# A bank rule in the list plan of a four-layer graph kernel, and less TensorE work in its first and last units

## The chip, the cores and the metric

The kernel runs on one core of a Trainium2 chip. The metric is the time on the device in microseconds (us), the median of three runs. Everything is computed in 32-bit floats.

The engines are named as in the profile: PE is the matrix engine (TensorE; PEld are its weight loads), DVE the vector engine, ACT the scalar engine, POOL GpSimd, and SP the engine that only issues transfers (DMAs). PSUM is the memory that PE writes its products to. It has eight banks of 128 x 512 floats; ACT and DVE read it.

## The reference

The input `x` has 64 graphs of 256 nodes with 128 features; one symmetric 0/1 matrix `adj` (256 x 256) is common to all. Four layers follow one another, each as `x = layernorm(x + layer(x))`:

- Layer 0: `h = x @ others_weight`; scores from sums of pairs of entries of `h @ a1` and `h @ a2`, leaky with 0.1, masked by `adj`, softmax over axis 1; the result is `att @ h + x @ self_weight`.
- Layer 1: `h = x @ W`; scores `leaky(h @ a_src + h @ a_dst)` for pairs of nodes, masked by `adj` with loops, softmax, `elu(attn @ h)`.
- Layer 2: five steps of a gated cell. In a step, `m = adj @ h` (it stands for both halves of the gate's input), `z` and `r` are sigmoids of `m` and `h`, `hv = tanh(m @ W5 + (r * h) @ U5)`, and `h = (1 - z) * h + z * hv`.
- Layer 3: `x @ W0 + sum over k = 1, 2, 3 of (adj^k @ x) @ (Wk + W(k+3))`.

## The kernel before

**Units and lanes.** Two graphs make a unit, so there are 32 units (`NU`), numbered from 0. A unit goes through layer 0 to 3 (`layer0` to `layer3`, lines 708 to 1176) on its own set of buffers, a lane. There are 10 lanes; a lane's next unit starts when its last one is done. So work of up to ten units is in flight.

**Feature-major and node-major.** Layer 2 needs the state turned from nodes-on-partitions to features-on-partitions and back in every step. There are two ways. On PE: four transposes into a bank (`feature_major`, L593; in the steps L1031) and one copy by ACT (L595, L1034). Or away from PE: one DVE transpose of 32 x 32 blocks (L606, L1006, L1019), one transfer to a buffer in DRAM (`hb`) and four back (L612, L1012). `far(u, step)` chooses: true is away from PE. `FIRST_FAR` gives the first step that is far in one of the first units, `LAST_FAR` the first that is not in one of the last, counted from the end (0 is unit 31). All other units are far in all steps.

**Products with adj.** After a far turn the product with `adj` is the fast one (`left_fast`, L885 to L939): three sums on POOL (L893 to L896), seven 128 x 128 products on PE (L904), two ACT copies (L916, L919), four DVE adds (L925 to L939). After a turn on PE it is the plain one (`left`, L881): four products of 256 columns and one ACT copy (L959). The gates follow (L963: products of 512 columns; L975, L984, L993: ACT; L978, L991, L996, L998: DVE).

**Loads of x.** Units below `XDIRECT` load `x` in one transfer (L364) and turn it on PE (L593, L595). The others load it in four transfers of quarter blocks with rows of 32 floats (L368) and turn it with one DVE transpose (L714).

**Layer 0's row terms.** For units below `DIRECT_D` the score's column term is computed on PE (four small products, L752); for the others a row is written to DRAM (`rowu`, L620), read back in two pieces (L743) and added (L746).

**Layer 3.** `layer3_blocks` (L1064 to L1146) computes it in 128 x 128 blocks: 21 products (L1088), POOL sums (L1080, L1121 to L1123), ACT copies (L1099) and DVE adds (L1102, L1135). The last `PLAIN` units use `layer3_end` (L1148 to L1172): 12 products of 256 columns (L1157, L1164) that hold two banks, two ACT copies (L1161). The last two units end with `layernorm_last` (L683 to L702).

**Dummy products.** `warm(WARM, ...)` puts products of the identity (L405) behind unit 0's layer 1, with the rank of a 33rd unit, so that they go only where PE has nothing else. Four more stand at the very start.

**The order.** `Plan` records every instruction as a task with an engine, an assumed duration, and what it reads and writes; then `Plan.run` lays out an order for all engines at once by simulating them: whenever an engine is free, it takes the ready task with the smallest key (`first`) among those for which there are free banks (`fits`). A key is the unit times `PERIOD` plus the task's due time; a due time adds up durations and latencies along what the task depends on, times `PACE` (`PACE_GATED` in layer 2). `HASTE` lowers the key of a task within the life of a bank that its unit holds, by engine. `START` is the time up to which other, shorter latencies are assumed; `TURN` delays a DVE instruction[...]; `MARGIN` lengthens assumed durations of an engine; `R2` and `R3` rank the setup of layers 2 and 3. The instructions are then issued in that order; the engines run it with the waits that the data and the banks need. Two tasks of one group (parts of one bank, say) have no dependence on each other in the plan.

Of the kernel before, what the change touches and what calls it, by code (L numbers as in the profile page):

```python
# [25 lines left out]
SMALL = ("ve", "cu", "d", "elu", "shift")  # L26
TIGHT = 4
HALVES = 0
DIRECT_D = 3
WARM = 6  # L30
FIRST_FAR = {0: 2, 1: 2}
LAST_FAR = {0: 1}
PERIOD = 41000.0
TAIL = 0.3
LATE = 5
PACE = 4.0
PACE_GATED = 1.56
HOLD = 80
DIRECT_ROWS = 3
XDIRECT = 10  # L40
START = 35e3
HASTE = {"pe": 45000.0, "act": 45000.0}
IN_PSUM = (0, 1, 0, 1)
MARGIN = {}
TURN = 12000.0
PLAIN = 4
R2 = 1
R3 = 1.5


class Cell:


    def __init__(self, ap=None, bank=False, over=(), seeded=False, full=False):
        self.ap, self.bank = ap, bank
        self.seeded, self.full = seeded, full

        self.over = list(over)
        for c in over:
            c.over.append(self)  # L60
        self.writers, self.readers, self.users = [], [], 0
        self.group, self.waits = None, set()


class Task:
# [9 lines left out]
class Plan:  # L75
# [2 lines left out]

    LATENCY = {"pe": 400, "dve": 350, "act": 350, "pool": 900, "sp": 4000}

    EARLY = {"pe": 250, "dve": 180, "act": 200, "pool": 250, "sp": 2500}
    OWN = {"pe": 0, "dve": 70, "act": 70, "pool": 100}
# [9 lines left out]
    def add(self, eng, ns, fn, reads=(), writes=(), after=(), wait=0, group=None, dma=False, port=False):  # L94
        dma = dma or eng == "sp"
        t = Task(eng, ns if dma or self.unit < 0 else ns * MARGIN.get(eng, 1.0), fn, self.unit, wait, dma)
        t.base = ns
# [25 lines left out]

    def seen_at(self, t, by):
        return t.end if t.eng != by.eng or t.dma else t.off + self.OWN[t.eng]

    def fits(self, t):
        seeded = sum(c.seeded for c in t.takes)
        return len(t.takes) <= len(self.free_banks) and seeded <= sum(self.full[id(b)] for b in self.free_banks)
# [26 lines left out]
    def run(self, spawn, units, key):  # L156

        queue, done_at, order = list(units), {}, []
        open_units, lane_of = {}, {}
        ready = {e: [] for e in ("pe", "dve", "act", "pool", "sp")}  # L160
        free = dict.fromkeys(ready, 0.0)
        held, twice = dict(dve=0.0, pool=0.0), False
        seen, now, running = 0, 0.0, []

        def enlist():
            nonlocal seen
            for t in self.tasks[seen:]:
                open_units[t.unit] = open_units.get(t.unit, 0) + 1
                t.left = 0
                for d in t.deps:  # L170
                    if d in done_at:
                        t.at = max(t.at, self.seen_at(d, t))
                    else:
                        t.left += 1
                        d.then.append(t)
                if not t.left:
                    ready[t.eng].append(t)
            seen = len(self.tasks)

        def start(lane):  # L180
            mine = [u for u in queue if u % LANES == lane]
            if mine:
                self.unit, self.step = mine[0], 0
                queue.remove(self.unit)
                lane_of[self.unit] = lane
                spawn(self.unit, lane)

                for t in self.tasks[seen:]:
                    t.due = max([d.due + (PACE_GATED if t.layer == 2 else PACE) * (d.ns + (
                        d.wait + self.LATENCY["sp" if d.dma else d.eng] if d.dma or d.eng != t.eng else self.OWN[t.eng]))  # L190
                        for d in t.deps if d.unit == t.unit], default=0.0)
                self.hold(self.tasks[seen:])
                enlist()

        enlist()
        for lane in range(LANES):
            start(lane)
        while any(ready.values()) or running:

            for t in [t for t in running if t.end <= now]:  # L200
                running.remove(t)
                for c in t.banks:
                    c.users -= 1
                    if not c.users:
                        self.full[id(c.ap)] = c.full
                        self.free_banks.append(c.ap)
                open_units[t.unit] -= 1
                if not open_units[t.unit] and t.unit in lane_of:
                    start(lane_of[t.unit])
            for e, tasks in ready.items():  # L210
                if free[e] > now:
                    continue

                fit = [t for t in tasks if t.at <= now + (HOLD if now < START else 0) and self.fits(t)]
                if not fit:
                    continue
                t = min(fit, key=lambda t: key(t) + (TURN if twice and t.port and e == "dve" else 0))
                if t.at > now:
                    continue
                tasks.remove(t)  # L220
                self.take(t)
                order.append(t)
                begin = now
                if t.port:
                    begin = max(now, held["pool" if e == "dve" else "dve"])
                free[e] = t.off = begin + t.ns
                if e == "dve":
                    twice = t.port
                if t.port:
                    held[e] = t.off - 65 if e == "dve" else begin + 50 if t.ns > 900 else t.off - 125  # L230
                t.end = t.off + (self.EARLY if now < START else self.LATENCY)["sp" if t.dma else e] + t.wait
                done_at[t] = t.end
                running.append(t)
                for n in t.then:
                    n.left -= 1
                    n.at = max(n.at, self.seen_at(t, n))
                    if not n.left:
                        ready[n.eng].append(n)
            times = [t.end for t in running] + [f for f in free.values() if f > now]
            times += [t.at for tasks in ready.values() for t in tasks if t.at > now]  # L240
            times = [x for x in times if x > now]
            if not times:
                assert not any(ready.values()), "the plan is stuck"
                break
            now = min(times)
        assert not queue and len(order) == len(self.tasks)
        return order
# [3 lines left out]
def kernel(  # L251
# [108 lines left out]
    def load_x(u, by="sp"):  # L360
        z = lanes[u % LANES]["m"]
        if u < XDIRECT:
            queue = {"sp": nc.sync, ACT: nc.scalar}[by]
# [69 lines left out]
    def blocks(name):  # L433

        whole = Cell(sb(name, [P, 2 * NC, N]))
        return whole, Cell(whole.ap[:, 0:NC])
# [63 lines left out]

    plan.rank = R2

# [41 lines left out]

    plan.rank = R3
    w3f, base = blocks("w3")
# [26 lines left out]
    def gd(ap):  # L573
        return ap.rearrange("p (g d) -> p g d", g=G)
# [10 lines left out]
    def far(u, step):  # L585


        return step >= FIRST_FAR.get(u, -1) and step < LAST_FAR.get(NU - 1 - u, STEPS + 1)

    def feature_major(src, view, t):  # L590
        ps = bank()
        for g in range(G):
            add(PE, 110, lambda g=g: nc.tensor.transpose(ps.ap[:, g * P : (g + 1) * P], view(g), ident.ap),  # L593
                (src, ident), (ps,))
        add(ACT, 475, lambda: nc.scalar.copy(t.ap, ps.ap), (ps,), (t,))  # L595
# [31 lines left out]
    def on_all(u, t, row, src, view):  # L627


        if u >= DIRECT_ROWS:  # L630
            to_row(row, src, view, G)
            from_row(t, row)
            return t, lambda: t.ap.rearrange("q (p b c) -> q b c p", b=UB, c=NC)
        ps = bank()
        for g in range(G):
            add(PE, 110, lambda g=g: nc.tensor.transpose(  # L636
                ps.ap[:, g * P : (g + 1) * P], view()[:, g : g + 1].to_broadcast([P, P]), ident.ap), (src, ident), (ps,))
        return ps, lambda: ps.ap.rearrange("q (b c p) -> q b c p", b=UB, c=NC)
# [70 lines left out]
    def layer0(u, L):  # L709
        xT, z = L["xT0"], L["m"]  # L710
        if u < XDIRECT:
            feature_major(z, lambda g: gd(z.ap)[:, g], xT)
# [23 lines left out]
        row, rv = on_all(u, lc, L["row"], cu, lambda: cu.ap[:, 2])  # L736
        if u >= DIRECT_D:
            to_row(L["rowu"], cu, lambda: cu.ap[:, 0:2].rearrange("p k g -> p (k g)"), 2 * G)
# [77 lines left out]
    def layer1(u, L):  # L816
# [48 lines left out]
        if not u:  # L865
            plan.rank = NU
            warm(WARM, [plan.tasks[-1]])
            plan.rank = None
# [177 lines left out]
    def layer3(u, L):  # L1046
# [10 lines left out]

        if u >= NU - PLAIN:
            layer3_end(u, L, xT, aT, s, tail)
# [123 lines left out]
    def first(t):  # L1183
        if t.rank is not None:
            return t.rank * PERIOD
        if t.unit < 0:
            return t.due - 1e6
        soon = HASTE.get(t.eng, 0) if t.within else 0
        return (t.unit if t.unit < NU - LANES else NU - 1 - LATE - (NU - 1 - t.unit) * TAIL) * PERIOD + t.due - soon
# [34 lines left out]
```

The softmax here doesn't subtract the row's maximum and nothing guards it: scores larger than these inputs give would overflow.

## Time and profile before

| what | us |
| --- | --- |
| median of 3 runs (1382.1 to 1382.66) | 1382.4 |
| the profiled execution | 1382.03 |
| its span, first to last instruction | 1380.2 |
| PE busy | 1371.9 |
| DVE busy | 1167.7 |
| ACT busy | 972.2 |
| POOL busy | 691.3 |

The granted clock of PE is 1.0 of its full speed. A group's row has line, engine, operation, output and inputs with their shapes, the count, then busy time in us, the mean of one in ns, then the idle time of the engine just before and what ended most of it. A 32-bit product is two matmul records in the trace, a transpose is one. Matmuls overlap in their pipeline, so that the mean of one is longer than the distance from one to the next. Numbers in tile names are left out: `ps` is any bank.

### The profile page before, as it was taken

What the parts mean: (1) busy time and instruction counts of PE and PEld (TensorE: products, weight loads), DVE (VectorE), ACT (ScalarE), POOL (GpSimd) and SP (SyncE); (2) the same over time, 40 slices, a digit from 0 to 9 for tenths busy, and PEclk for the clock granted to TensorE, in tenths of its full rate; (3) what the DMA queues carried; (4) which work ended last, traced back from release to release, by engine and by line L of the source; (5) the groups of instructions that cost most, each with busy time, mean ns of one, the idle gap of its engine ahead of it and who ended that gap; (6) DMA issues with size and microseconds to landing.
All of it is one profiled execution on the core that took longest, in us unless ns stands there. A gap on an engine that the chain in (4) does not pass through costs nothing.

```text
span 1380.2 us, 24466 instructions
## 1 busy us (share of the span) xinstructions
PE 1371.9 (99%) x7221; PEld 970.5 (70%) x7221; DVE 1167.7 (85%) x2709; ACT 972.2 (70%) x2414; POOL 691.3 (50%) x1240
## 2 busy tenths in 40 slices
PE   9999999999999999999999999999999999999998
PEld 9767676676676776767767667776666676667777
DVE  7968988988888888899888998888888787889854
ACT  6897676756776777778777767788766656566555
POOL 5214473544554664556545564565545433446814
PEclk9999999999999999999999999999999999999999
DMA  4223454454455455454555455545555443645412
GB/s 128 56 55 89 105 117 114 98 126 106 107 131 108 92 117 137 109 118 105 109 126 119 112 111 110 109 107 134 119 114 117 90 103 84 131 111 117 109 47 69
DMA packets 530084, 147.21 MB, mean 107 GB/s; under 512 B 456480, under 2 KB 495136, under 8 KB 529952
## 3 DMA queue, kind: packets, MB, share of 16 engines
q1 hardware_dynamic: 529152, 145.13, 46.8%
q8 instruction: 58, 0.95, 0.3%
q14 instruction: 74, 0.61, 0.2%
q10 hardware_dynamic: 800, 0.52, 0.1%
HBM read 81.10 MB, written 64.46 MB: 105 GB/s over the span
## 4 chain that ended last, share of the span: by engine, by line
PE 98%; DVE 1%; ACT 0%; issue 0%; POOL 0%; POOLq 0%; DVEq 0%; ACTq 0%
PE ps L963 50%; PE ps L904 20%; PE ps L1088 10%; PE ps L840 4%; PE ps L803 4%; PE ps L727 2%; PE ps L852 2%; PE ps L798 2%; PE ps L881 1%; PE ps L1157 1%; PE ps L1164 0%; PE ps L405 0%; PE ps L593 0%; PE ps L1031 0%; PE ps L636 0%; PE ps L752 0%
## 5 line engine op out<-in xcount | busy, mean ns | idle before, releaser
L963 PE MATMUL ps<-m,gT 128*128 128x512 f32 x960 | 473.3, 593 | 0.0
L963 PEld LDWEIGHTS ps<-m,gT 128*128 128x128 f32 x960 | 168.0, 191 | 131.8 <-issue 114.4
L975 ACT ACTIVATE e<-ps,bias 128x512 f32<-128x512 f32 x160 | 109.8, 687 | 94.7 <-PE ps L963 85.8
L649 POOL TENSOR_SCALAR ve<-st 128x4 f32<-128x4 f32 x110 | 26.8, 244 | 278.4 <-DVE st L647 269.6
L963 PE MATMUL ps<-e,u5T 128*128 128x512 f32 x320 | 163.5, 592 | 0.0
L904 PEld LDWEIGHTS ps<-adjTp,ht 128*128 128x128 f32 x726 | 118.6, 191 | 61.2 <-issue 48.6
L652 POOL TENSOR_TENSOR rstd<-ve,nhalf 128x4 f32<-128x4 f32 x126 | 137.5, 1091 | 47.5 <-DVE ve L649 41.4
L993 ACT ACTIVATE p<-ps,bias 128x512 f32<-128x512 f32 x160 | 109.9, 687 | 66.6 <-PE ps L963 64.2
L904 PE MATMUL ps<-adjTp,e 128*128 128x128 f32 x968 | 149.0, 276 | 0.2 <-ACT m L919 0.2
L984 ACT ACTIVATE ps<-ps,bias 128x512 f32<-128x512 f32 x160 | 105.6, 661 | 55.1 <-PE ps L963 54.3
L893 POOL TENSOR_TENSOR e<-ht 128x256 f32<-128x256 f32 x121 | 96.9, 801 | 88.1 <-DMA ht<-hb 73.1
L904 PEld LDWEIGHTS ps<-adjTp,e 128*128 128x128 f32 x968 | 129.6, 192 | 11.9 <-issue 7.9
L996 DVE SCALAR_TENSOR_TENSOR ps<-ps,p 128x512 f32<-128x512 f32 x160 | 110.2, 689 | 32.0 <-ACT p L993 31.4
L904 PE MATMUL ps<-adjTp,ht 128*128 128x128 f32 x726 | 136.7, 275 | 0.0
L963 PEld LDWEIGHTS ps<-e,u5T 128*128 128x128 f32 x320 | 58.7, 190 | 63.1 <-issue 55.5
L963 PE MATMUL ps<-xT,gT 128*128 128x512 f32 x192 | 98.2, 593 | 0.0
L671 ACT ACTIVATE x<-ht,ve,rstd 128x128 f32<-128x128 f32 x208 | 91.1, 490 | 5.1 <-POOL ve L660 5.0
L936 DVE TENSOR_TENSOR m<-ps,m 128x256 f32<-128x256 f32 x182 | 74.8, 413 | 14.1 <-PE ps L904 12.8
L829 ACT ACTIVATE e<-m,esd 128x256 f32<-128x256 f32 x116 | 84.6, 769 | 0.0
L978 DVE SCALAR_TENSOR_TENSOR e<-e,xT 128x512 f32<-128x512 f32 x96 | 72.2, 752 | 12.9 <-ACT e L975 12.4
L893 POOL TENSOR_TENSOR e<-x 128x256 f32<-128x256 f32 x61 | 48.6, 797 | 65.5 <-ACT x L671 57.7
L919 ACT COPY m<-ps 128x128 f32<-128x128 f32 x182 | 48.0, 268 | 44.0 <-PE ps L904 35.0
(219 smaller groups left out, 3356.1 us busy)
## 6 DMA issues: line engine op xcount, KB each, us to landing
hb<-p SPq DMA_DIRECT2D x182, 256.0 KB, 2.3
ht<-hb SPq DMA_DIRECT2D x484, 64.0 KB, 2.6
xT<-hb SPq DMA_DIRECT2D x244, 64.0 KB, 2.6
m<-row SPq DMA_DIRECT2D x58, 256.0 KB, 3.7
hb<-p SPq DMA_DIRECT2D x124, 64.0 KB, 1.8
ht<-hb SPq DMA_DIRECT2D x31, 256.0 KB, 2.8
out_dram<-x SPq DMA_DIRECT2D x30, 256.0 KB, 2.4
m<-in_x_dram SPq DMA_DIRECT2D x88, 64.0 KB, 2.4
```

What stands on the lines that cost most here:

```text
L652: add(POOL, 1010, lambda: nc.gpsimd.tensor_tensor(rstd.ap, ve.ap, nhalf.ap, op=ALU.pow), (ve, nhalf), (rstd,))
L671: add(ACT, 400, lambda j=j, b=b, ch=ch, view=view, at=at, shift=shift, col=col: nc.scalar.activation(X[u].ap[:, b, ch, :], view()[:, j, :] ...
L829: add(ACT, 660 if u >= DIRECT_ROWS else 360, lambda g=g, b=b: nc.scalar.activation(e.ap[:, g, :].rearrange("p (c n) -> p c n", c=NC), ev() ...
L893: add(by, wide, lambda: eng.tensor_sub(four[:, 0:2], blk(slice(2, 3)).to_broadcast([P, 2, D]), blk(slice(0, 4, 3))), (src,), (s,), group=s ...
L904: add(PE, mm_ns(P) + 4, lambda: nc.tensor.matmul(ps.ap[:, at * P : (at + 1) * P], lhs(), mat.ap[:, k, c * P : (c + 1) * P], start=start, s ...
L936: add(DVE, 335, lambda: nc.vector.tensor_tensor(mv[:, 1:3], pv(y)[:, 0:2], mv[:, 3:4].to_broadcast([P, 2, P]), op=ALU.add), (y, m), (m,))
L963: add(PE, mm_ns(T), lambda: nc.tensor.matmul(ps.ap, w(), rhs.ap, start=start, stop=stop, skip_group_check=True), (c, rhs), (ps,), after)
L975: add(ACT, 590, lambda ps_g=ps_g, up=up, tr=tr: nc.scalar.activation(tr.ap, ps_g.ap, AF.Tanh, bias=bias2.ap[:, 1:2], scale=0.5 / up), (ps_ ...
L984: add(ACT, 590, lambda ps_g=ps_g, up=up, tz=tz: nc.scalar.activation(tz.ap, ps_g.ap, AF.Tanh, bias=bias2.ap[:, 0:1], scale=0.5 / up), (ps_ ...
L993: add(ACT, 590, lambda ps_v=ps_v, up=up, tv=tv: nc.scalar.activation(tv.ap, ps_v.ap, AF.Tanh, bias=bias2.ap[:, 2:3], scale=1 / up), (ps_v, ...
L996: add(DVE, 600, lambda tz=tz, tv=tv, vv=vv: nc.vector.scalar_tensor_tensor(vv.ap, tz.ap, 1.0, tv.ap, op0=ALU.add, op1=ALU.mult), (tv, tz), ...
L1088: nc.tensor.matmul(part(ps, at)[:, 0], l(), r(), start=start, stop=True, skip_group_check=True)
```

## The change

The planner gets a rule: a task that uses a bank is taken only when no instruction of another engine that used this bank (as far as it is the same cell, one use of a bank from its first writer to its last reader) is still unfinished in the simulated time. Each cell keeps the end of the last task of each engine (`last`), and `settled` asks for it. Apart from that, constants change: which turns and which products stay on PE in the first and last units, how `x` of units 5 to 9 is loaded and turned, how unit 2's column term is computed, which form layer 3 has in units 28 and 29, how many dummy products there are, and the constants of the order. The order of all engines is laid out anew from them.

```diff
-DIRECT_D = 3
-WARM = 6
-FIRST_FAR = {0: 2, 1: 2}
-LAST_FAR = {0: 1}
+DIRECT_D = 2
+WARM = 3
+FIRST_FAR = {0: 2, 1: 1}
+LAST_FAR = {0: 3}
 PERIOD = 41000.0
 TAIL = 0.3
 LATE = 5
-PACE = 4.0
+PACE = 3.0
 PACE_GATED = 1.56
 HOLD = 80
 DIRECT_ROWS = 3
-XDIRECT = 10
-START = 35e3
-HASTE = {"pe": 45000.0, "act": 45000.0}
+XDIRECT = 5
+START = 25000.0
+HASTE = {"pe": 70000.0, "act": 70000.0, "dve": 70000.0}
 IN_PSUM = (0, 1, 0, 1)
-MARGIN = {}
-TURN = 12000.0
-PLAIN = 4
-R2 = 1
-R3 = 1.5
+MARGIN = {"pool": 1.1}
+TURN = 1000.0
+PLAIN = 2
+R2 = 1.3
+R3 = 2.0
...
         self.group, self.waits = None, set()
+        self.last = {}
...
-    LATENCY = {"pe": 400, "dve": 350, "act": 350, "pool": 900, "sp": 4000}
+    LATENCY = {"pe": 400, "dve": 350, "act": 350, "pool": 900, "sp": 3500}
...
+    def settled(self, t, now):
+
+        return not any(e != t.eng and end > now for c in t.banks for e, end in c.last.items())
+
...
-                fit = [t for t in tasks if t.at <= now + (HOLD if now < START else 0) and self.fits(t)]
+                fit = [t for t in tasks if t.at <= now + (HOLD if now < START else 0) and self.fits(t) and self.settled(t, now)]
...
                 done_at[t] = t.end
+                for c in t.banks:
+                    c.last[e] = t.end
```

## The prediction

> **What bounds the kernel now.** I read the page's busy line and the chain that ended last, then a table of stages, then the order of TensorE (PE) in the first and last units, and last the groups of waits on ACT and DVE. First the page:
>
> ```profile
> span 1380.2 us, 24466 instructions
> ...
> PE 1371.9 (99%) x7221; PEld 970.5 (70%) x7221; DVE 1167.7 (85%) x2709; ACT 972.2 (70%) x2414; POOL 691.3 (50%) x1240
> ...
> PE 98%; DVE 1%; ACT 0%; issue 0%; POOL 0%; POOLq 0%; DVEq 0%; ACTq 0%
> ```
>
> PE is busy for all but 8.3 us of the span and is 98% of the chain. Busy can hide a stall, so I also took the distance from one matmul record's start to the next: a 512-column record steps 0.429 us (chain row: L963 x16 in 6.87), a 256-column one 0.216 (L881 x16 in 3.46), a 128-column one 0.111 (L904 x16 in 1.78), a transpose 0.11 (L1031 below: 4 from 1351.62 to 1352.06). An f32 product is two such records, a transpose one. All 7221 records at those steps come to about 1366 us. With 1.3 us before the first matmul and 5.6 after the last one's end (1374.65), about 7 us of stalls are left: 3 in the first 10 us, some 4 in the remaining 1364. So PE's order has almost nothing left to give; what PE no longer has to do is the only large term. The stages (columns: length, then busy PE, PE load, DVE, ACT, POOL, clock, DMA share, GB/s):
>
> ```profile
> 10.00:20.00 10.00, 10.00 (x90) 9.87 (x87) 9.23 (x28) 6.24 (x21) 8.56 (x20) 1.00 0.75 207
> 20.00:30.00 10.00, 10.00 (x92) 10.00 (x91) 8.65 (x31) 7.83 (x24) 6.08 (x12) 1.00 0.04 4
> 30.00:36.00 6.00, 5.93 (x45) 5.49 (x44) 4.54 (x17) 4.64 (x15) 2.01 (x2) 1.00 0.35 75
> 36.00:48.00 12.00, 12.00 (x82) 10.99 (x81) 11.97 (x39) 10.50 (x29) 3.81 (x8) 1.00 0.17 31
> 48.00:60.00 12.00, 12.00 (x58) 8.47 (x57) 11.69 (x34) 10.70 (x30) 1.51 (x2) 1.00 0.34 67
> ...
> 1340.00:1370.00 30.00, 30.00 (x158) 25.19 (x157) 15.61 (x42) 15.52 (x39) 13.95 (x31) 1.00 0.21 54
> ```
>
> DVE is full from 36 to 60 us, and PE full beside it; at the end PE is full and DVE half idle. PE's own order in the first units and near the end:
>
> ```profile
> 28.53 1.91 PE L593 MATMUL ps<-ident,m 128*128 128x128 f32 x16
> ...
> 36.35 3.79 PE L727 MATMUL ps<-wx,xT 128*128 128x133 f32 x32
> 39.97 1.03 PE L405 MATMUL ps<-ident 128*128 128x256 f32 x4
> ...
> 42.67 0.59 PE L405 MATMUL ps<-ident 128*128 128x256 f32 x2
> ...
> 1351.62 0.60 PE L1031 MATMUL ps<-ident,p 128*128 128x128 f32 x4
> ```
>
> L405 is the dummy product with the lowest rank: from 40 to 48 us PE had nothing else ready. So the "full" PE of 36 to 48 us is filled, partly with dummies, partly with the first work of units 6 to 9 (L593, L727), while DVE sets the pace.
>
> **What the Trainium skill says.** "PSUM — Partial Sum Buffer", section on bank collisions: two engines may not use one bank at once, even at different columns, and have to be kept apart by bank. The trace agrees: the groups below wait for an instruction with which they share a bank and no data (L671 and L808 both read layer 0's product; L925 and L919 both read the bank x of the fast product). "TensorE: Matmul & The Clock Gate", section "Wait — 56ns, not 53.3ns?": N/2.4 + 2.5 ns a matmul; the 0.429 us of a 512-column record is that with the columns passed twice (426.7 + 2.5). "Perfetto Trace Analysis", section "Identifying the Most-Contended Engine": matmul busy share tells little of headroom; hence the start-to-start account above. "DMA: Bandwidth & Descriptors", section "Why small descriptors are slow (HBM only)": small pieces cost an overhead each; the turned load reads rows of 128 bytes where the plain one reads 512, and the DMA share is already 0.75 at 10 to 20 us.
>
> ```profile
> L671 ACT ACTIVATE x<-ps,ones,rstd 128x128 f32<-128x128 f32 x112 | 44.9, 463 | 8.5 <-DVE esd L808 5.7 <-POOL rstd L652 2.2 <-DVE ht L873 0.5
> L919 ACT COPY m<-ps 128x128 f32<-128x128 f32 x182 | 48.0, 268 | 44.0 <-PE ps L904 35.0 <-DVE m L925 8.0
> L925 DVE TENSOR_TENSOR m<-ps,e 128x128 f32<-128x128 f32 x182 | 50.5, 281 | 33.1 <-PE ps L904 19.0 <-ACT m L919 12.6
> ```
>
> **The change, part by part.**
>
> XDIRECT 10 to 5: units 5 to 9 lose 4 PE transposes each, 20 x 0.11 = 2.20 us of PE, and a copy on ACT, 5 x 0.588 = 2.9. They gain a DVE transpose (L714, 0.699), 5 x 0.70 = 3.5 us, and four 64 KB loads for one of 256 KB: 15 more issues on SP at about 0.5 us (L368 x2 in 1.01), so SP ends its loads at about 22 us and not 14.7. DVE's idle time from 10 to 36 us is 26 - 22.4 = 3.6 us, just the 3.5 that is added, if the loads are there in time; otherwise it lands in the stretch in which DVE is full.
>
> DIRECT_D 3 to 2: unit 2 loses 8 records at 0.107 (8 from 11.32 to 12.18), 0.86 us of PE. Its score goes by rowu (lands in 1.8), then two reads of it (3.0), queued behind those loads: d at 22 + 0.5 + 1.8 + 1.2 + 3.0, about 29 us, where DVE's L766 of unit 2 now starts at 22.8. What is late next is its max, exponential and product L803 (32.8 and 35.5 now), about 6 us; the rows of unit 3 (27.5 now) are behind the same loads but after 22.
>
> WARM 6 to 3: 6 records x 0.216 = 1.30 us of PE that only fills.
>
> FIRST_FAR of unit 1 and LAST_FAR of unit 31: three turns less on PE, 12 x 0.11 = 1.32 us. Three plain products (8 x 0.216 = 1.73) become fast ones (14 x 0.111 = 1.55): 3 x 0.17 = 0.52. ACT loses three copies of 0.59 and three of 0.58 and gains six of 0.27; DVE gains 3 x (0.70 + 0.28 + 0.41 + 0.28 + 0.41) = 6.2, POOL 3 x 1.9, SP 3 x 5 issues. At the end DVE and POOL have room; for unit 1, at about 70 us, DVE is at 31 of 40 us. Latency of a turn: 0.7 on DVE, 2.3 to land in hb, 2.6 for the last of four reads, with about 2.5 of issue, some 8 us for 1.4 before; the fast product is about 2 longer than the plain one.
>
> PLAIN 4 to 2: units 28 and 29 take the block form, 42 x 0.112 = 4.70 for 24 x 0.216 = 5.18: 2 x 0.48 = 0.96 us. More copies, adds and POOL sums, on engines that are half idle there.
>
> The bank rule (settled, last) and the constants of the order (PACE, START, HASTE, TURN, MARGIN, R2, R3, the latency of SP) remove no instruction. The waits that the rule foresees exist already, 26 us on ACT and DVE in the rows above, but off PE's path. On PE all stalls from 100 to 1300 us come to about 4 us net; a better order may gain 3 of them, and a worse one has no natural end: 1% of the span is 14 us. I take a gain of 0.5.
>
> Sum of PE work: 2.20 + 0.86 + 1.30 + 1.32 + 0.52 + 0.96 = 7.16 us. Of it 4.36 (first three) lies before 48 us, where PE is partly filled, and 2.80 where PE is full of work. The 2.80 I count whole. Of the 4.36 the dummies' 1.30 buys nothing (idle in their place), and of the other 3.06 I count 2.2: those transposes and products stood in PE's order ahead of real work, but less filler means some new idle time. So 2.80 + 2.2 + 0.5 = 5.5 us: span 1374.7; with the 1.8 us around it (1382.03 - 1380.2) 1376.5; the median is 0.4 above that run, so 1376.9, say **1377**.
>
> **Rivals.** A difference of 0.2%, 2.8 us, is about what a measurement tells from none: faster is under 1379.6, slower over 1385.2.
>
> (1) Everything counts and stalls shrink too: 7.2 + 2.5, 1372.7. For it: the order knows waits it did not know. Against: it knew nearly nothing of them and PE still lost only 4 us.
>
> (2) The head takes back what was removed there: PE idles for the 4.4 us, and L727 of units 5 to 9 (32 records, 3.6 us at 36 us) comes later since x is turned later, leaving another 0 to 3.6 us open. Then 2.8 less 0 to 3.6: 1379.6 to 1383.2, no difference. For it: the dummies at 40 to 48 us and DVE at 11.97 of 12. Here also the case that the bank rule changes only waits that PE never feels.
>
> (3) Slower, by the tail: unit 31's steps end now at 1310.8, 1323.7, 1337.7, 1351.7 (its transposes), 13 to 14 us a step, and each step has only about 2 us of slack (its PE, ACT and DVE work in a row is near 9 us and ten hand-overs of about 0.3 are 3). Two turned steps add about 2 x (6.6 + 2) = 17 us to this chain. It costs nothing while unit 31 is started that much earlier and layer 3 of other units (L1088, L1157) fills PE. If it isn't, PE runs dry at the end: the slide is 17 less what the earlier start and some 8 us of slack absorb; from 8.3 us of slide on (5.5 + 2.8) the kernel is slower, at 17 it is 1394. Against it: at 1340 to 1370 PE is without a gap, so fill exists.
>
> (4) Slower, by a worse middle: stalls of 9 us or more in place of 4, 1386 to 1390.
>
> **How the numbers follow.** The forecast's own case 0.42 (1374 to 1379.6), rival 1 0.18, rival 2 0.18, rival 3 0.12, rival 4 0.10. Faster 0.60, same 0.18, slower 0.22. The range leaves out about half of the cases 3 and 4 at the top and a little of 1 at the bottom: 1371.5 to 1387.
>
> **What would show it.** PE records go from 7221 to 7229: 20 + 8 + 6 + 12 fewer, and 3 x (14 - 8) and 2 x (42 - 24) more, short ones for long ones, with PE busy about 1365. L593 has 32 records, L405 14, L752 16, L881 56, L1157 32, L1031 20, L714 27 on DVE. Right: no PE gap in the last 70 us and under 3 us of new idle time before 60 us. Wrong: PE below 90% at 20 to 50 us (rival 2), after 1330 us (rival 3), or PE waits spread from 100 to 1300 us (rival 4). A head that runs faster because unit 0's chain got a better order would beat the forecast.

## The result and the profile after

The changed kernel takes 1374.7 us (1374.17 to 1375.07, four runs) against 1382.5 us (four runs) before: a ratio of 0.9944, 95% interval 0.9926 to 0.9961. That is 7.8 us less, clear of the noise, inside the range, and 2.3 us below the forecast. The page of the changed kernel (lines after the added code are 7 higher: L970 was L963):

```profile
span 1373.3 us, 24671 instructions
...
PE 1361.0 (99%) x7229; PEld 964.4 (70%) x7229; DVE 1181.2 (86%) x2744; ACT 965.5 (70%) x2419; POOL 701.0 (51%) x1263
...
PE 96%; DVE 2%; ACT 1%; SPq 1%; DMA 0%; issue 0%; POOL 0%; POOLq 0%; DVEq 0%
```

PE is still 99% busy and nearly the whole chain. Nothing in this page tells where 7 us of span went, so one account is used from here on, worked out from the start times of all matmul records of a trace. The *step* of a record is what it takes in a dense row (its columns twice at 2.4 GHz plus 2.6 ns, at least 111 ns for 128 columns); the sum of all steps is *PE's work*. A start more than 25 ns later than the step before it allows is a *late start*; how late these starts are is added up by stage. A late start can be a wait or a step at a lower clock. The rest are late starts below 25 ns, about 3 us in each kernel, and the 1.3 us before the first matmul. Of the first stage, 3.0 us before and 2.6 after lie in the first 10 us, where the first records of 256 columns step 0.427 us.

| kernel (profiled run), us | PE's work | late, 0-60 | late, 60-400 | late, 400-1300 | late, after 1300 | after last matmul | span |
| --- | --- | --- | --- | --- | --- | --- | --- |
| before | 1359.6 | 3.7 | 0.9 | 5.6 | 0.5 | 5.6 | 1380.2 |
| after | 1352.3 | 7.7 | 0.0 | 2.1 | 0.1 | 6.7 | 1373.3 |

So 7.3 us of work went, the first 60 us took 4.0 back, the rest of the order gave 4.8 (0.9 + 3.5 + 0.4), and the end took 1.1: 7.0 of span. (This profiled run is the slowest of its four, and that of before, 1382.03, lies below the four that it is compared with: hence 7.8 in the medians.) From 100 to 1300 us, 52 starts were late before, by 6.6 us in all and none by more than 0.54; after, 8 are, by 2.1 us, half of it one wait for the transfer of a turn (in the table of PE's waits: total us, times, longest):

```profile
PE ps L911 <- DMA ht<-hb: 0.9, 1, 0.9
```

The stages after:

```profile
36.00:48.00 12.00, 10.63 (x62) 8.42 (x60) 11.93 (x40) 9.42 (x29) 4.69 (x7) 1.00 0.41 99
48.00:60.00 12.00, 11.25 (x51) 7.90 (x52) 12.00 (x35) 12.00 (x35) 0.40 (x2) 1.00 0.14 41
...
1340.00:1370.00 30.00, 26.57 (x169) 23.29 (x168) 16.41 (x52) 18.79 (x53) 16.59 (x34) 1.00 0.24 62
```

At 36 to 48 us PE has 1.4 us of open gaps beside a full DVE, where it had none; at 48 to 60 us ACT is full as well (in the last row PE simply ends at 1366.6). PE's order there:

```profile
37.37 1.46 PE L412 MATMUL ps<-ident 128*128 128x256 f32 x6
...
41.69 2.06 PE L810 MATMUL ps<-ht,p 128*128 128x130 f32 x16 [1.08 <-DVE ht L792]
...
48.75 0.65 PE L643 MATMUL ps<-ident,esd 128*128 128x128 f32 x4 [1.04 <-DVE esd L815]
```

The filler of units 6 to 9 (L734, L727 before) is used up by 35 us; then come the three dummies, then PE waits for DVE. The waits for an engine that shares a bank and no data, in the table of waits after (total us, times, longest):

```profile
ACT m L926 <- DVE m L932: 6.8, 9, 2.0
DVE m L932 <- ACT m L926: 0.8, 3, 0.3
DVE esd L815 <- ACT x L678: 0.4, 2, 0.3
```

Before they were 8.0, 12.6 and 1.7 us, and 5.7 of ACT for esd, which has gone: 28.0 us fell to 8.0. So the plan does what it says.

### The profile page after: what moved, and what is told of

The parts are those of the page before. It is cut to its first block, busy times and chain, and to the rows that moved or that the text cites. A ratio compares the mean times of both kernels' runs of the same rounds, so it can differ in the third digit from the quotient of the medians.

```text
span 1373.3 us, 24671 instructions
## 1 busy us (share of the span) xinstructions
PE 1361.0 (99%) x7229; PEld 964.4 (70%) x7229; DVE 1181.2 (86%) x2744; ACT 965.5 (70%) x2419; POOL 701.0 (51%) x1263
## 4 chain that ended last, share of the span: by engine, by line
PE 96%; DVE 2%; ACT 1%; SPq 1%; DMA 0%; issue 0%; POOL 0%; POOLq 0%; DVEq 0%
PE ps L970 49%; PE ps L911 21%; PE ps L1095 10%; PE ps L810 4%; PE ps L847 4%; PE ps L805 2%; PE ps L859 2%; PE ps L734 2%; PE ps L888 1%; PE ps L1164 1%; DVE st L654 0%; SPq L619 0%; PE ps L412 0%; DVE e L765 0%; DMA xT<-hb 0%
## 5 line engine op out<-in xcount | busy, mean ns | idle before, releaser
L970 PE MATMUL ps<-m,gT 128*128 128x512 f32 x960 | 479.2, 593 | 0.0
L970 PEld LDWEIGHTS ps<-m,gT 128*128 128x128 f32 x960 | 165.7, 191 | 119.4 <-issue 100.6
L659 POOL TENSOR_TENSOR rstd<-ve,nhalf 128x4 f32<-128x4 f32 x126 | 133.7, 1061 | 64.6 <-DVE ve L656 53.1
L970 PE MATMUL ps<-e,u5T 128*128 128x512 f32 x320 | 163.5, 592 | 0.0
L911 PE MATMUL ps<-adjTp,e 128*128 128x128 f32 x992 | 153.8, 275 | 0.0
L911 PEld LDWEIGHTS ps<-adjTp,e 128*128 128x128 f32 x992 | 133.9, 192 | 11.1 <-issue 10.5
L911 PE MATMUL ps<-adjTp,ht 128*128 128x128 f32 x744 | 140.1, 275 | 0.9 <-DMA ht<-hb 0.9
L656 POOL TENSOR_SCALAR ve<-st 128x4 f32<-128x4 f32 x110 | 30.9, 281 | 193.7 <-DVE st L654 185.3
L970 PEld LDWEIGHTS ps<-e,u5T 128*128 128x128 f32 x320 | 58.7, 190 | 62.7 <-issue 51.4
L678 ACT ACTIVATE x<-ht,ve,rstd 128x128 f32<-128x128 f32 x216 | 95.1, 492 | 5.1 <-POOL ve L667 4.3
L970 PE MATMUL ps<-xT,gT 128*128 128x512 f32 x192 | 98.3, 593 | 0.4 <-DMA xT<-hb 0.4
L943 DVE TENSOR_TENSOR m<-ps,m 128x256 f32<-128x256 f32 x185 | 76.3, 414 | 9.9 <-PE ps L911 8.6
L946 DVE TENSOR_TENSOR m<-ps,m 128x256 f32<-128x256 f32 x185 | 75.8, 413 | 1.1
```

Source lines behind the costliest of these rows:

```text
L659: add(POOL, 1010, lambda: nc.gpsimd.tensor_tensor(rstd.ap, ve.ap, nhalf.ap, op=ALU.pow), (ve, nhalf), (rstd,))
L678: add(ACT, 400, lambda j=j, b=b, ch=ch, view=view, at=at, shift=shift, col=col: nc.scalar.activation(X[u].ap[:, b, ch, :], view()[:, j, :] ...
L911: add(PE, mm_ns(P) + 4, lambda: nc.tensor.matmul(ps.ap[:, at * P : (at + 1) * P], lhs(), mat.ap[:, k, c * P : (c + 1) * P], start=start, s ...
L943: add(DVE, 335, lambda: nc.vector.tensor_tensor(mv[:, 1:3], pv(y)[:, 0:2], mv[:, 3:4].to_broadcast([P, 2, P]), op=ALU.add), (y, m), (m,))
L970: add(PE, mm_ns(T), lambda: nc.tensor.matmul(ps.ap, w(), rhs.ap, start=start, stop=stop, skip_group_check=True), (c, rhs), (ps,), after)
```

## The experiments

**Theories.** A: the bank rule removed the late starts in the middle. B: the new constants of the order did. C: any new order differs by chance. Each kernel here makes the order anew, so each is also a draw; two of them change nothing but that, and their expectations name this D. Diffs over several lines are given in short form, and late starts are those of one execution of each kernel.

*The rule alone out of the changed kernel:*

```diff
-... and self.fits(t) and self.settled(t, now)]
+... and self.fits(t)]
```

> The changed kernel with the bank rule alone taken out of the planner; all constants stay. Theory A (the rule removed the stalls in the middle): the matmul steps from 100 to 1300 us again hold about 4.6 us more stall than in the changed kernel (net excess -0.8 there, +3.8 before), so 1374.7 + 4.6 = 1379.3 us. Theory B (the constants of the order did it): middle as in the changed kernel, 1374 to 1376 us. Theory C (any new order differs by chance): anywhere from 1373 to 1380 us, with the stalls at other places.

Measured 1392.4 us (ratio to before 1.0068, 1.0051 to 1.0085). This is above all three theories. The late starts from 100 to 1300 us grow by 7.3 us, where A said 4.6, but head and end grow with them. The bank waits are back at 22.9 us (9.0, 5.2, 6.6, 2.1).

*The rule alone into the kernel before:*

```diff
-... and self.fits(t)]
+... and self.fits(t) and self.settled(t, now)]
```

> The kernel before with the bank rule alone put in; all constants stay. Theory A: the middle loses its 3.8 us of net stall and head and tail stay, 1382.5 - 4.6 = 1378 us. Theory B: no change, 1381.5 to 1383.5 us, with some 50 stalls over 25 ns between 100 and 1300 us as before. Theory C: 1378 to 1386 us.

Measured 1389.4 us (1.0051, 1.0036 to 1.0066): slower, against all three. The bank waits fell to 8.0 us all the same (4.6, 0.9, 0.9, 1.6). So these waits are not what PE's late starts hang on by themselves.

*Only the six constants that take work off PE, in the kernel before:*

```diff
-DIRECT_D = 3, WARM = 6, FIRST_FAR[1] = 2, LAST_FAR = {0: 1}, XDIRECT = 10, PLAIN = 4
+DIRECT_D = 2, WARM = 3, FIRST_FAR[1] = 1, LAST_FAR = {0: 3}, XDIRECT = 5, PLAIN = 2
```

> The kernel before with only the six constants that take work off PE (DIRECT_D, WARM, FIRST_FAR, LAST_FAR, XDIRECT, PLAIN); no rule, old constants of the order. All theories: PE's ideal work falls by 7.4 us. If the head takes back what is removed there (4.1 us more stall before 60 us, as in the changed kernel), and the middle keeps its stalls: 1382.5 - 7.4 + 4.1 + about 1 of tail = 1380 us. If the head only idles because of the new order, 1375 us.

Measured 1413.6 us (1.0225, 1.0209 to 1.0240), 33 us above what was expected. PE's work is down by the same 7.3 us, and the kernel is 31 us slower: 10.2 us of late starts in the head, 23.5 at the end. The end is the prediction's tail rival, in PE's order of this kernel (L1031 and L593 are unit 31's transposes):

```profile
1386.69 1.02 PE L963 MATMUL ps<-e,u5T 128*128 128x512 f32 x2
1390.01 0.66 PE L1031 MATMUL ps<-ident,p 128*128 128x128 f32 x4 [2.30 <-DVE p L998]
1394.64 1.63 PE L593 MATMUL ps<-ident,x 128*128 128x128 f32 x4 [3.98 <-ACT x L671]
1396.07 2.83 PE L881 MATMUL ps<-adjT,x 128*128 128x256 f32 x8
```

Unit 31 is alone at the end, and PE waits for its last step (2.30) and its normalization (3.98). In the changed kernel the step's transposes stand at 1350.93, with layer 3 of other units around them, and the late starts after 1300 us sum to 0.1 us.

*Only the constants of the order, in the kernel before:*

```diff
-PACE 4.0, START 35e3, HASTE pe, act 45000, MARGIN {}, TURN 12000, R2 1, R3 1.5, sp 4000
+PACE 3.0, START 25e3, HASTE pe, act, dve 70000, MARGIN pool 1.1, TURN 1000, R2 1.3, R3 2.0, sp 3500
```

> The kernel before with only the constants of the order (PACE, START, HASTE, TURN, MARGIN, R2, R3, the latency of SP); no rule, and PE's work as before. Theory A: the middle keeps about 4 us of net stall, 1382 us. Theory B: the middle loses them, 1378 us. Theory C: 1378 to 1386 us.

Measured 1390.3 us (1.0057, 1.0042 to 1.0072), mostly in the head (9.4 us late). None of the three had it.

*Nothing but an order made anew, after and before:*

```diff
-PERIOD = 41000.0
+PERIOD = 41200.0
```

> The changed kernel with PERIOD 41200 in place of 41000 (0.5%): same rule, same work, same other constants, only an order made anew. Theory D (each order is a draw: the stalls of an order hang on small things, and the kernel as changed stands at a good draw): PE's work stays, the stalls grow by 5 to 15 us at other places, 1379 to 1390 us. Theory A' (rule and constants together make good orders as such): within 2 us of the changed kernel, 1373 to 1377 us.

> The kernel before with PERIOD 41200 in place of 41000: only an order made anew. Theory D: 1387 to 1395 us, like the single parts of the change. Theory A': within 2 us of the kernel before, 1380.5 to 1384.5 us.

Measured 1376.1 us on the changed kernel and 1392.5 us on the kernel before (1.0072, 1.0055 to 1.0088). The first follows A', the second D: 0.5% in one constant costs the kernel before 10 us, with 8.2 us of late starts at the end. Beside this one neighbour, its order was a lucky one.

*The head's three constants set back in the changed kernel:*

```diff
-DIRECT_D = 2, WARM = 3, XDIRECT = 5
+DIRECT_D = 3, WARM = 6, XDIRECT = 10
```

> The changed kernel with the head's three constants set back (XDIRECT 10, DIRECT_D 3, WARM 6): 4.4 us more PE work before 48 us. By the account of the head (4.1 us more stall in the changed kernel took back what was removed): the work comes back, the stalls before 60 us fall from 7.6 to about 3.6, the rest as in the changed kernel, so 1375 us. If those stalls come from the new order: 1379 us. Theory D adds 5 to 15 us of stalls anywhere.

Measured 1378.9 us (0.9974, 0.9963 to 0.9984). The late starts before 60 us fall from 7.7 to 4.5, as expected; but 2.6 us come up at 100 to 400 us, and the total is where the other theory had it. So the removed 4.4 us of head work do cost some 3.2 in late starts, and the order's draw decides what remains.

*The tail's two constants set back in the changed kernel:*

```diff
-LAST_FAR = {0: 3}, PLAIN = 2
+LAST_FAR = {0: 1}, PLAIN = 4
```

> The changed kernel with the tail's two constants set back (LAST_FAR {0: 1}, PLAIN 4): 2.2 us more PE work in the last units (8 transposes 0.88, two plain products 0.34, two units of layer 3 0.96). The sum made for the prediction: 1374.7 + 2.2 = 1376.9 us with no gap at the end. Theory D adds 5 to 15 us of stalls anywhere.

Measured 1376.0 us (0.9954, 0.9939 to 0.9969), 1.3 over the changed kernel and not 2.2: the time after the last matmul is 5.5 us here and 6.7 there, which returns most of the difference. The chain that ended last, of the changed kernel (start, us, what), shows why:

```profile
1364.66 0.52 DVE ht L1109 x2
1365.17 0.68 DVE st L654 x2
...
1367.74 1.65 ACT x L678 x4
1369.39 0.22 ACT x L703
```

A unit in block form (L1109) now ends last but one, and its four normalizations on ACT (L678) stand ahead of the last unit's (L703), which starts 0.7 us after its input is there (DVE L701, 1368.39 to 1368.55).

*Rule and order constants in the kernel before, PE's work as it was:*

```diff
-... and self.fits(t)], PACE 4.0, START 35e3, HASTE pe, act 45000, and so on
+... and self.fits(t) and self.settled(t, now)], PACE 3.0, START 25e3, HASTE pe, act, dve 70000, and so on
```

> The kernel before with the rule and all constants of the order, and PE's work as before (the six constants of the work stay old). If rule and order constants make a clean middle by themselves: stalls from 100 to 1300 us as low as in the changed kernel (4.8 us by this account, floor 2.8), 1382.4 - 4.5 = 1378 us. If the constants fit only the whole set that they stand in: stalls of 8 to 12 us or more in the middle, 1386 to 1392 us.

Measured 1386.3 us (1.0031, 1.0019 to 1.0043). The total says that the set doesn't fit this work. But the late starts lie at 100 to 400 us (5.5) and at the end (3.2); from 400 to 1300 us they are 1.1 us. So the steady part is as good without the new work constants.

*Unit 2's column term back on PE:*

```diff
-DIRECT_D = 2
+DIRECT_D = 3
```

> The changed kernel with DIRECT_D 3: unit 2's score goes by PE again (0.86 us more PE work at 15 to 20 us) and no longer waits for the row behind the loads. Its DVE instruction that needs d starts near 23 us and not at 32.9. By the account of the head, the two PE stalls that follow (1.25 us at 40.3 us, for the scaled h of unit 2; 1.19 us at 47.1 us) vanish: stalls before 60 us fall from 7.6 to about 5. The middle is a new draw: total 1373 if it stays clean, up to 1384 if it doesn't.

Measured 1378.9 us (0.9973, 0.9963 to 0.9984). The term is early again (L773 of unit 2 starts at 22.2 us), and the two waits are gone, but others have come in the same stretch of PE's order:

```profile
28.51 1.18 PE L734 MATMUL ps<-wx,xT 128*128 128x133 f32 x8 [1.21 <-DVE xT L721]
...
42.87 1.46 PE L412 MATMUL ps<-ident 128*128 128x256 f32 x6
45.95 1.99 PE L847 MATMUL ps<-p,x 128*128 128x256 f32 x8 [1.62 <-DVE p L840]
```

The head is late by 8.4 us and not by 5: unit 2's late term is not what keeps the head late. The waits shown are for DVE here too, and L721 is one of the DVE transposes that the change moved there.

*No dummies at all:*

```diff
-WARM = 3
+WARM = 0
```

> The changed kernel with WARM 0: the last three dummy products go (1.30 us of PE), and the order of everything else can stay. The prediction's term (dummies taken out buy nothing): 1374.7 us, 1.3 us more stall before 60 us. If they had stood in the way of work: 1373.4 us.

Measured 1374.2 us (1373.88 to 1374.64), the changed kernel within their spreads. The head's late starts rise from 7.7 to 8.9 us, nearly by the 1.3 us of work that went. Where the three dummies stood, PE now waits (its order in this kernel):

```profile
38.37 1.16 PE L859 MATMUL ps<-wx,xT 128*128 128x129 f32 x8 [0.84 <-ACT xT L850]
```

*POOL's margin, 10% to 1.9%:*

```diff
-MARGIN = {"pool": 1.1}
+MARGIN = {"pool": 1.019}
```

> The changed kernel with POOL's assumed durations lengthened by 1.9% and not by 10%: only the order is made anew. If the stalls that are left (7.6 us in the head, about 2 above the floor in the middle, 1.1 us more tail) depend on the fit of the constants, a better fit can take some 2 to 3 us more: 1371.5 to 1373 us. If 1374.7 is near what PE's work allows, no change, 1374 to 1376 us.

Measured 1373.8 us (1373.09 to 1374.67; ratio to before 0.9937, 0.9924 to 0.9951): lowest of all medians, though its interval overlaps that of the changed kernel, so a gain is not shown. Its late starts are 6.8 us in the head and 0.2 from 400 to 1300 us.

**All kernels side by side** (us, profiled runs; late starts of over 25 ns, medians in the last column):

| kernel | rule | order constants | late, 0-60 | late, 60-400 | late, 400-1300 | late, after 1300 | median |
| --- | --- | --- | --- | --- | --- | --- | --- |
| before | no | old | 3.7 | 0.9 | 5.6 | 0.5 | 1382.4 |
| PERIOD, before | no | old | 4.0 | 2.1 | 7.8 | 8.2 | 1392.5 |
| work only | no | old | 10.2 | 7.5 | 6.5 | 23.5 | 1413.6 |
| order constants only | no | new | 9.4 | 2.9 | 4.8 | 1.1 | 1390.3 |
| rule taken out | no | new | 10.0 | 3.0 | 6.4 | 9.3 | 1392.4 |
| rule only | yes | old | 7.1 | 2.0 | 7.9 | 0.9 | 1389.4 |
| rule and order constants | yes | new | 4.5 | 5.5 | 1.1 | 3.2 | 1386.3 |
| after | yes | new | 7.7 | 0.0 | 2.1 | 0.1 | 1374.7 |
| PERIOD, after | yes | new | 8.1 | 0.5 | 1.4 | 2.1 | 1376.1 |
| head undone | yes | new | 4.5 | 2.6 | 1.4 | 1.1 | 1378.9 |
| tail undone | yes | new | 7.8 | 0.0 | 1.3 | 0.7 | 1376.0 |
| DIRECT_D 3 | yes | new | 8.4 | 3.5 | 1.4 | 0.3 | 1378.9 |
| WARM 0 | yes | new | 8.9 | 0.0 | 0.9 | 0.1 | 1374.2 |
| POOL margin | yes | new | 6.8 | 0.1 | 0.2 | 0.0 | 1373.8 |

Two things can be read here. In the steady part, 400 to 1300 us, the eight kernels with the rule and the new constants are late by 0.2 to 2.1 us, whatever else they do, and the six without one or the other by 4.8 to 7.9. The gap between the two groups is some 5 us on the mean, and it needs both: the rule with the old constants has 7.9, the new constants without the rule 4.8 and 6.4. The bound at 400 us was set after the runs; from 100 to 1300 us, the stage of the expectations, the groups nearly touch (0.3 to 6.5 and 6.6 to 13.9). In the first 400 us and after 1300 us there is no such order. There the rule with the new constants leaves anything from 6.9 to 11.9 us late before 400 and 0.0 to 3.2 after 1300, the others 4.6 to 17.7 and 0.5 to 23.5; small edits move it by several us.

## Why the prediction was right, and where it was not

**PE's work.** Right: 7.16 us forecast, 7.3 found, and every count as stated (7229 records in all; L593 32, L405 14, L752 16, L881 56, L1157 32, L1031 20, L714 27, by their old lines). Only PE's busy time, forecast at about 1365 us, came to 1361.0. This term is the same in every kernel with the six constants, the one of 1413.6 us among them: it is the one part of the change that no order can take away, and it is not enough by itself.

**"Of the 4.36 ... I count 2.2".** Too much. The head took back 4.0 us of 4.36; rival 2 had it as "PE idles for the 4.4 us". The sign that the prediction named for being right, under 3 us of new idle time before 60 us, did not come. The dummies' 1.30 bought nothing, as said: the last three, taken out alone, come back as 1.2 us. The other 3.06 bought about 0.3 from before to after, or 1.2 by the run that sets the head back within the changed kernel (3.2 us for 4.4). Most of the removed transposes were filler for PE, as the dummies were. That DVE sets the pace there is a reading of its busy time (11.93 of 12 us and 12.00 of 12) and of PE's two longest waits; no run makes DVE faster to test it, and ACT is full too from 48 us on. How much of the new waiting comes from the later x, and how much from the five DVE transposes, no run tells apart; that unit 2's late term is not it, the run with DIRECT_D 3 shows. Its delay itself was as worked out: d forecast for about 29 us, found at 31.2.

**"I take a gain of 0.5" for the order.** This is the step that failed, by size. The order gave 4.8 us, of which some 3.5 lie in the steady part and hold in all eight kernels of the kind. The base was short: at the steps that the prediction lists, the 7221 records come to 1358.6 us and not to "about 1366", so that about 14 us were open and not 7. From 100 to 1300 us, late starts alone were 6.6 us, not "about 4 us net", and the change left 2.1. PE's order had more to give than "almost nothing". The argument "the waits that the rule foresees ... off PE's path" looked at each wait alone. They are off PE's path, and the rule cut them by 20 us without helping PE in the kernel with the rule only. What was left out is the partner: with the constants that were put beside the rule (which of them, no run tells: they were changed together), PE's starts become reliable in the steady part. The 2.5 us of rival 1 were nearer. That the total still lies in the forecast's own case (1374 to 1379.6) is in part luck: the gain of the order made up for the loss in the head. And the draw has a share in it, as 0.5% in PERIOD cost the kernel before 10 us, and the changed kernel with either edit in the head takes 1378.9.

**The end.** "No PE gap in the last 70 us" was right, with 0.1 us late. The 1.1 us after the last matmul was not foreseen: layer 3 in block form ends on ACT ahead of the last unit.

**The rivals.** Rival 2 was right about the head and not about the total, since it gave the order nothing. Rival 3 did not come, but the mechanism is real: with the old order the same work constants gave 23.5 us late at the end, where the prediction had priced a chain of 17 us longer. It was right to name it and to say that it hangs on whether unit 31 is started earlier. Rival 4 did not come either; the kernel before was nearer to it than the changed one, as 0.5% in PERIOD shows.

Errors of size thus went both ways: 1.9 us too good for the head, 4.3 too poor for the order, 1.1 too good for the end, 1.3 left in the span. The 0.4 that was added for the median was 0.4 the other way, since this profiled run lies above its median: that is most of the rest.

## What to carry to other kernels

Work taken from the engine that bounds the whole is a gain only in the stages that it bounds: here 3.2 to 4.0 of the 4.4 us removed in the first 48 us came back as waiting, while 1.3 of the 2.2 us removed from the last units show in the time. An order laid out by a planner is to be judged by several neighbours of it, since one constant moved by 0.5% may cost ten us; what holds in all neighbours (here the steady part) belongs to the rule with its constants, the rest may be the draw. Parts of such a change are tried together too: each of the three (rule, work, order constants) alone was slower than no change, in the one order that each was given.

## What the runs showed of the hardware

In the kernel with the work constants only, PE waits 3.98 us near the end and comes back at half clock. Its stages there (the third figure from the right is the granted clock):

```profile
1386.00:1390.00 4.00, 1.71 (x4) 0.40 (x3) 2.08 (x3) 1.35 (x2) 0.00 (x0) 1.00 0.00 0
1390.00:1394.00 4.00, 0.66 (x4) 0.42 (x4) 1.45 (x3) 0.00 (x0) 1.56 (x4) 0.64 0.00 0
1394.00:1396.00 2.00, 1.36 (x4) 0.75 (x5) 0.00 (x0) 1.65 (x4) 0.06 (x1) 0.50 0.00 0
1396.00:1398.00 2.00, 2.00 (x6) 1.64 (x6) 0.00 (x0) 0.59 (x1) 0.00 (x0) 0.51 0.00 0
1398.00:1400.00 2.00, 2.00 (x10) 1.77 (x10) 0.00 (x0) 0.59 (x1) 0.00 (x0) 1.00 0.00 0
```

In smaller stages of this trace the clock is 1.00 from 1390 to 1391.1 us, 0.50 from 1391.2 to 1397.9 and 1.00 after 1398: full clock returns some 3.4 us after PE's restart at 1394.64. In between, 256-column records step 0.43 us in place of 0.216, which costs about 1.1 us. The four transposes step 0.39 in place of 0.11, but for another reason: each waits for its part of the normalization on ACT, which does four in 1.65 us:

```profile
1394.10 1.65 ACT L671 ACTIVATE x<-m,ve,rstd 128x128 f32<-128x128 f32 x4 [5.60 <-POOL ve L660]
...
1395.03 0.18 PEld L593 LDWEIGHTS ps<-ident,x 128*128 128x128 f32 x1 [0.20 <-ACT x L671]
```

The Trainium skill has the fall of the clock ("TensorE: Matmul & The Clock Gate", section "What's actually happening": half rate after an idle window of about 3.4 us). The trace agrees in part: the clock fell only 0.5 us into the gap of 3.98 us, and the 3.4 us before the fall were not wholly idle, as they held four transposes (0.66 us). The tail rival's price had left this out: the gap costs itself and about 1.1 us more. It is not the only one. The clock is 0.50 also from 1363.9 to 1370.6 us of this kernel, where slower steps make up some 2.9 of the 23.5 us of late starts. So once PE runs dry, part of what is lost comes after the wait.
